# Turning the convolution's products round: conv matrices as the stationary side, result by channel

## The chip, the cores and the metric

One core of one Trainium2 chip. The metric is device time in microseconds (us), the median of several executions. The kernel before took 2316.77 us in the median of 3 runs (2316.7 to 2318.37).

## The reference, cut to what matters

64 graphs of 256 nodes with 256 channels, all in f32, go through a gated graph layer and a second graph layer. The part that the change touches is the convolution branch of the first layer:

```python
xc = jnp.transpose(x, (0, 2, 1))
h = jax.nn.relu(_bn(_conv1d(xc, conv1_w, 0), bn1_g, bn1_b, bn1_m, bn1_v))
h = _bn(_conv1d(h, conv2_w, 8), bn2_g, bn2_b, bn2_m, bn2_v)      # 17 taps
x_conv = jnp.transpose(jax.nn.relu(h + xc), (0, 2, 1))
s = x @ w_se.T + b_se                                            # distances, messages ...
A = jnp.exp(-dist) * mask
msg = jax.nn.relu(x @ w_msg.T + b_msg)
...                                                              # gates (GRU) on [x_conv, A @ msg], norm, second layer
```

## The kernel before

The 17-tap convolution is done for eight elements at once, as a transform on VectorE, 47 products of 256 x 256 with prepared matrices `w2m` on TensorE, and an inverse transform on VectorE. The data stand on the stationary side, so the result has positions on the partitions. The gates need channels there, so after x was added the result was transposed on TensorE, and ScalarE's relu wrote it to `xc`:

```python
def product(ps, slot, w, m):
    for c in range(C):
        nc.tensor.matmul(ps, X[:, slot, c * P:(c + 1) * P], w(m, c), start=(c == 0), stop=(c == C - 1))
...
def products(b, first, sums):                  # one group: 6 products into three PSUM banks
    p1, p2, p3 = bank("ps_k1"), bank("ps_k2"), bank("ps_k3")
    ...
    def take():                                # the group's evacuation
        k1 = sl(sums, 2).rearrange("p s e -> p (s e)")
        nc.scalar.copy(k1, p1)
        nc.vector.tensor_sub(..., k1, p3)
        nc.vector.tensor_add(..., k1, p2)
    return take
...
# the tail of conv(b)
before = []
for q in range(4):
    xb = x_by_tiles(b, q)
    nc.vector.tensor_add(sl(V + 4 * q, 4), sl(V + 4 * q, 4), xb)
    yield cost(4)
    yield None
    before.append(channels(q))                 # 8 transposes, 4 relus, two times "yield 1.0"
    if len(before) > 2:
        yield from before.pop(0)
...
```

The convolution of block b+1 is put between the work of the elements of block b. `conv` is a generator. Each `yield` says what the step just emitted counts for. Ten times in each element, 80 times in a block, `pump` draws steps from it until the sum drawn has reached its share of `total`, which is what all the steps of one block sum to:

```python
POINTS = 10
...
done, at, goal = 0.0, 0, BG * POINTS - 6

def pump():
    nonlocal done, at
    at += 1
    while done < total * at / goal:
        t = next(coming, 1e9)
        if t is None:
            break
        done += t

for k in range(b * BG, (b + 1) * BG):
    ...
    project(k - 1)
    step(up)                    # state update, part 1: two DVE operations, tanh
    pump()
    distances(k + 2)
    step(up)                    # part 2: three 128x512 operations and the norm's statistics on DVE
    pump()
    messages(k + 3)
    step(up)
    pump()
    ...
```

These calls emit each engine's instructions in this order, and the traces show what hangs on it: in the changed kernel a subtraction on DVE (L394, shown below) started 4.7 us after the copy that it needs was done, behind the part of a state update that stood before it.

## Time and profile before

| | per steady block (730.6 to 1003.2 us) | share |
|---|---|---|
| block | 272.6 us | |
| TensorE (PE) busy | 269.5 us | 99% |
| VectorE (DVE) busy | 208.5 us | 76% |
| ScalarE (ACT) busy | 89.8 us | 33% |

How to read it: a block lasts from the first gate of its first element (the first matmul of `ps_rz`) to that of the next. In the trace of before these gates start at 190.2, 458.8, 730.6, 1003.2, 1275.7, 1547.1, 1818.3 and 2089.9 us. So the front takes 190.2, seven blocks take 271.4 on average, and the last block, which carries no convolution, takes 224.7 to the end.

### The profile page before, as it was taken

What the parts mean: (1) busy time and instruction counts of PE and PEld (TensorE: products, weight loads), DVE (VectorE), ACT (ScalarE), POOL (GpSimd) and SP (SyncE); (2) the same over time, 40 slices, a digit from 0 to 9 for tenths busy, and PEclk for the clock granted to TensorE, in tenths of its full rate; (3) what the DMA queues carried; (4) which work ended last, traced back from release to release, by engine and by line L of the source; (5) the groups of instructions that cost most, each with busy time, mean ns of one, the idle gap of its engine ahead of it and who ended that gap; (6) DMA issues with size and microseconds to landing.
All of it is one profiled execution on the core that took longest, in us unless ns stands there. A gap on an engine that the chain in (4) does not pass through costs nothing.

```text
span 2314.6 us, 24215 instructions
## 1 busy us (share of the span) xinstructions
PE 2225.2 (96%) x8262; PEld 1456.2 (63%) x8262; DVE 1685.2 (73%) x3212; ACT 766.0 (33%) x1577; POOL 468.7 (20%) x925
## 2 busy tenths in 40 slices
PE   7879999999999999999999999999999999999996
PEld 4565566666666666666666566665666656666663
DVE  2893998759794788829887498956889398874543
ACT  4514222442224321353224332253223532243332
POOL 1000221312122222202212131221222122121211
PEclk8998999999999999999999999999999999999998
DMA  5543152224323144221532234222433214321100
GB/s 176 156 161 114 59 170 67 85 94 130 118 73 109 50 137 132 74 100 37 169 99 73 101 106 143 75 96 69 136 105 101 94 43 151 113 78 37 46 23 14
DMA packets 211128, 226.66 MB, mean 98 GB/s; under 512 B 22087, under 2 KB 201790, under 8 KB 211006
## 3 DMA queue, kind: packets, MB, share of 16 engines
q1 hardware_dynamic: 188448, 191.14, 26.2%
q10 hardware_dynamic: 22558, 33.99, 4.2%
q8 instruction: 66, 1.08, 0.2%
q14 instruction: 56, 0.46, 0.1%
HBM read 179.22 MB, written 45.88 MB: 97 GB/s over the span
## 4 chain that ended last, share of the span: by engine, by line
PE 69%; DVE 21%; DMA 4%; issue 3%; POOL 2%; ACT 1%; ACTq 0%; SPq 0%; DVEq 0%; POOLq 0%
PE ps_rz L637 14%; PE ps_k L383 12%; DVE XF L103 8%; PE ps_n L649 7%; PE ps_rz L635 7%; PE ps_out L712 6%; PE ps_c L454 5%; PE ps_nmp L619 4%; PE ps_n L647 4%; PE ps_out L724 3%; PE ps_msg L575 3%; DVE w L103 2%; DVE XF L464 2%; DVE bst L654 2%; DMA w<-w2m 2%
## 5 line engine op out<-in xcount | busy, mean ns | idle before, releaser
L103 DVE SCALAR_TENSOR_TENSOR XF<-XF 128x512 f32<-128x512 f32 (+2 forms) x800 | 506.7, 664 | 7.0
L676 POOL TENSOR_SCALAR q<-mv 128x2 f32<-128x2 f32 x64 | 32.1, 502 | 1459.1 <-DVE mv L655 1459.1
L383 PE MATMUL ps_k<-w,XF 128*128 128x256 f32 x1316 | 302.1, 385 | 15.2 <-ACT AT L609 11.6
L383 PEld LDWEIGHTS ps_k<-w,XF 128*128 128x128 f32 x1316 | 248.5, 192 | 64.1 <-ACT AT L609 17.3
L650 DVE TENSOR_TENSOR gn<-ps_n,brzn 128x512 f32<-128x512 f32 x128 | 88.1, 688 | 239.4 <-PE ps_n L649 239.4
L641 ACT ACTIVATE rz<-rz 128x512 f32<-128x512 f32 x128 | 80.7, 631 | 509.9 <-DVE rz L640 509.9
L635 PE MATMUL ps_rz<-whh,xT 128*128 128x512 f32 x512 | 240.8, 592 | 0.0
L637 PE MATMUL ps_rz<-wih,xc 128*128 128x512 f32 x512 | 240.6, 592 | 0.0
L637 PE MATMUL ps_rz<-wih,nmp 128*128 128x512 f32 x512 | 240.6, 592 | 0.0
L712 PE MATMUL ps_out<-wrr,hT 128*128 128x512 f32 x512 | 232.8, 598 | 5.5 <-ACT hT L701 5.5
L640 DVE TENSOR_TENSOR rz<-ps_rz,brzn 128x512 f32<-128x512 f32 x128 | 87.2, 681 | 192.2 <-PE ps_rz L637 192.2
L637 PEld LDWEIGHTS ps_rz<-wih,nmp 128*128 128x128 f32 x512 | 97.3, 190 | 122.5 <-issue 122.5
L637 PEld LDWEIGHTS ps_rz<-wih,xc 128*128 128x128 f32 x512 | 97.2, 190 | 122.5 <-issue 121.5
L712 PEld LDWEIGHTS ps_out<-wrr,hT 128*128 128x128 f32 x512 | 98.1, 192 | 105.2 <-issue 89.6
L580 ACT ACTIVATE msg<-msg 128x512 f32<-128x512 f32 x64 | 40.4, 631 | 353.1 <-DVE msg L579 353.1
L575 PE MATMUL ps_msg<-wms,xT 128*128 128x260 f32 x512 | 134.1, 402 | 12.5 <-DMA adj<-in_adjT_dram 8.1
L635 PEld LDWEIGHTS ps_rz<-whh,xT 128*128 128x128 f32 x512 | 92.2, 190 | 64.5 <-issue 61.2
L647 PE MATMUL ps_n<-whh,xT 128*128 128x256 f32 x512 | 131.6, 379 | 0.0
L649 PE MATMUL ps_n<-wih,xc 128*128 128x256 f32 x512 | 131.4, 379 | 0.0
L649 PE MATMUL ps_n<-wih,nmp 128*128 128x256 f32 x512 | 131.4, 379 | 0.0
L360 DVE TENSOR_TENSOR XF<-XF 128x512 f32<-128x512 f32 (+3 forms) x128 | 125.2, 1004 | 1.8
L454 PE MATMUL ps_c<-xTc,w 128*128 128x512 f32 x256 | 118.1, 604 | 7.6 <-ACT xTc L446 7.6
(105 smaller groups left out, 3486.6 us busy)
## 6 DMA issues: line engine op xcount, KB each, us to landing
w<-w2m SPq DMA_DIRECT2D x105, 768.0 KB, 5.9
xn<-in_x_dram SPq DMA_DIRECT2D x32, 512.0 KB, 4.3
xt<-xTc ACTq DMA_DIRECT2D x32, 512.0 KB, 3.3
xT<-xt SPq DMA_DIRECT2D x64, 256.0 KB, 3.0
adj<-in_adjT_dram SPq DMA_DIRECT2D x64, 256.0 KB, 2.8
x<-in_x_dram SPq DMA_DIRECT2D x64, 256.0 KB, 3.1
xb<-in_x_dram SPq DMA_DIRECT2D x32, 512.0 KB, 4.9
out_dram<-y ACTq DMA_DIRECT2D x64, 256.0 KB, 2.2
```

Source lines behind the costliest of these rows:

```text
L103: nc.vector.scalar_tensor_tensor(o, in0, s, in1, op0=op0, op1=op1)
L360: (nc.vector.tensor_add if add else nc.vector.tensor_sub)(sl(o, n), sl(a, n), sl(b, n))
L383: nc.tensor.matmul(ps, X[:, slot, c * P:(c + 1) * P], w(m, c), start=(c == 0), stop=(c == C - 1))
L454: nc.tensor.matmul(ps, w1[:, c, o * P:(o + 1) * P], xTc[:, c, :], start=(c == 0), stop=(c == C - 1))
L575: nc.tensor.matmul(ps[:, :D + 4], XT[k][:, c, m * P:(m + 1) * P], wms[:, c, :], start=(c == 0), stop=(c == C - 1))
L619: nc.tensor.matmul(ps[:, d * N:(d + 1) * N], MSG[k][:, m, d * P:(d + 1) * P], AT[k][:, m, :], start=(m == 0), stop=(m == C - 1))
L635: nc.tensor.matmul(prz, XT[k][:, c, q], whh[:, c, 0:2 * D], start=(c == 0), stop=False)
L637: nc.tensor.matmul(prz, t, wih[:, i, 0:2 * D], start=False, stop=(i == 3))
L647: nc.tensor.matmul(pn[:, D:], XT[k][:, c, q], whh[:, c, 2 * D:], start=(c == 0), stop=(c == C - 1))
L649: nc.tensor.matmul(pn[:, :D], t, wih[:, i, 2 * D:], start=(i == 0), stop=(i == 3))
L650: nc.vector.tensor_add(RZ[k][1][:, n, :], pn, brzn[:, 2 * D:])
L712: nc.tensor.matmul(ps, hT[:, c, n * P:(n + 1) * P], wrr[:, c, :], start=(c == 0), stop=(c == C - 1))
```

## The change

Its intent: put the conv matrix on the stationary side and the data on the moving side. Then the product comes out with channels on the partitions, and the 256 transposes of the result are not needed. x is added from the copy that already lies transposed in DRAM, and the batch norm's shift becomes the bias of the relu.

```diff
     def product(ps, slot, w, m):
-        for c in range(C):
-            nc.tensor.matmul(ps, X[:, slot, c * P:(c + 1) * P], w(m, c), start=(c == 0), stop=(c == C - 1))
+        for o in range(C):
+            q = slice(o * P, (o + 1) * P)
+            for c in range(C):
+                nc.tensor.matmul(ps[:, q], w(m, c)[:, q], X[:, slot, c * P:(c + 1) * P],
+                                 start=(c == 0), stop=(c == C - 1))
 ...
-                for j in range(4):
-                    nc.tensor.transpose(ps[:, j * P:(j + 1) * P], X[:, V + 4 * q + j, o * P:(o + 1) * P], ident)
-                ...
-                yield 1.0
-        before = []
-        for q in range(4): ...
+        def add_x(pair):
+            xb = conv_pool.tile([P, C, 2 * N], F32, tag="xb", name="xb")
+            nc.sync.dma_start(out=xb, in_=xt_dram[b * BG // 2 + pair])
+            v = view[:, :, :, pair * 2 * M:(pair + 1) * 2 * M]
+            nc.vector.tensor_add(v, v, xb.rearrange("p c (r j) -> p j c r", j=M))
+            yield cost(4)
+        def channels(pair):
+            for o in range(C):
+                nc.scalar.activation(xcs[h][:, o, g:g + 2]..., view[...], AF.Relu, bias=bn_shift[1][:, o:o + 1])
+        for pair in range(BG // 2):
+            yield from add_x(pair)
+            channels(pair)
 ...   (cut: x_by_tiles, the shift's row and its add in last_products)
```

The eight `yield 1.0` went with the transposes. They stood for 8 of the 107.7 units in `total`.

More of the change, by code (lines that the diff above doesn't have):

```diff
@@ L113, in weight @@
         return t
-    def x_by_tiles(b, q):
-        t = conv_pool.tile([P, 4, D], F32, tag="xb", name="xb")
-        nc.sync.dma_start(
-            out=t, in_=x[b * BG:(b + 1) * BG].rearrange("g (t j) d -> (g t) j d", j=M)[:, 4 * q:4 * q + 4, :])
-        return t
     chan_sb = const.tile([P, 8, C], F32)
@@ L139, in gnn_two_layers @@
     bn_scale, bn_shift = [], []
-    bn2_row = const.tile([P, 2, D], F32)
+    bn2_row = const.tile([P, D], F32)
     def batch_norms():
@@ L155, in along_rows @@
     def along_rows(pool):
-        for i, v in enumerate((bn_scale[1], bn_shift[1])):
-            ps = bank("ps_row")
-            for c in range(C):
-                dg = pool.tile([P, P], F32, tag="dg", name="dg", bufs=4)
-                nc.vector.tensor_scalar(dg, ident, v[:, c:c + 1], None, ALU.mult)
-                nc.tensor.matmul(ps[:, c * P:(c + 1) * P], ones, dg, start=True, stop=True)
-            nc.scalar.copy(bn2_row[:, i, :], ps[:, :D])
+        ps = bank("ps_row")
+        for c in range(C):
+            dg = pool.tile([P, P], F32, tag="dg", name="dg", bufs=2)
+            nc.vector.tensor_scalar(dg, ident, bn_scale[1][:, c:c + 1], None, ALU.mult)
+            nc.tensor.matmul(ps[:, c * P:(c + 1) * P], ones, dg, start=True, stop=True)
+        nc.scalar.copy(bn2_row, ps[:, :D])
     w2m = tc.dram_tile([NM, C, P, D], F32, name="w2m")
@@ L192, in scaled @@
                 ws[:, :n], WT[i][:, :, o - o0:o - o0 + n * OB].rearrange("p k (b o) -> p b k o", o=OB),
-                bn2_row[:, 0, o:o + n * OB].rearrange("p (b o) -> p b o", o=OB).unsqueeze(2)
+                bn2_row[:, o:o + n * OB].rearrange("p (b o) -> p b o", o=OB).unsqueeze(2)
                 .to_broadcast([P, n, TAPS, OB]))
@@ L381, in product @@
     def product(ps, slot, w, m):
-        for c in range(C):
-            nc.tensor.matmul(ps, X[:, slot, c * P:(c + 1) * P], w(m, c), start=(c == 0), stop=(c == C - 1))
+        for o in range(C):
+            q = slice(o * P, (o + 1) * P)
+            for c in range(C):
+                nc.tensor.matmul(ps[:, q], w(m, c)[:, q], X[:, slot, c * P:(c + 1) * P],
+                                 start=(c == 0), stop=(c == C - 1))
     def products(b, first, sums):
@@ L415, in take @@
             nc.scalar.copy(X[:, S2 + 6, :], p1[:, :D])
-            nc.scalar.copy(X[:, U + 1, :], p3[:, D:])
+            nc.scalar.copy(X[:, U:U + 2, :].rearrange("p s e -> p (s e)"), p3)
             nc.vector.tensor_sub(X[:, U + 2, :], X[:, S2 + 6, :], p2[:, :D])
             nc.vector.tensor_add(X[:, U + 3, :], X[:, S2 + 6, :], p1[:, D:])
-            nc.vector.tensor_add(X[:, U, :], p3[:, :D], bn2_row[:, 1, :])
         return take
@@ L522, in conv @@
         xcs = [work.tile([P, C, 4, N], F32, tag="xc", name="xc", bufs=3) for _ in range(2)]
-        def channels(q):
-            for o in range(C):
-                ps = bank("ps_xc")
-                for j in range(4):
-                    nc.tensor.transpose(ps[:, j * P:(j + 1) * P], X[:, V + 4 * q + j, o * P:(o + 1) * P], ident)
-                pv = ps.rearrange("p (j g t) -> p j g t", j=4, g=BG)
-                for h in range(2):
-                    nc.scalar.activation(
-                        xcs[h][:, o].rearrange("p g (t j) -> p j g t", j=M)[:, 4 * q:4 * q + 4],
-                        pv[:, :, 4 * h:4 * h + 4, :], AF.Relu)
-                yield 1.0
-        before = []
-        for q in range(4):
-            xb = x_by_tiles(b, q)
-            nc.vector.tensor_add(sl(V + 4 * q, 4), sl(V + 4 * q, 4), xb)
-            yield cost(4)
-            yield None
-            before.append(channels(q))
-            if len(before) > 2:
-                yield from before.pop(0)
-        for c_ in before:
-            yield None
-            yield from c_
+        view = X[:, V:V + M].rearrange("p j (c r t) -> p j c (r t)", c=C, r=BG)
+        def add_x(pair):
[5 more added lines that the diff above has]
+        def channels(pair):
+            h, g = pair // 2, 2 * (pair % 2)
+            for o in range(C):
+                nc.scalar.activation(
+                    xcs[h][:, o, g:g + 2].rearrange("p g (t j) -> p j g t", j=M),
+                    view[:, :, o, pair * 2 * M:(pair + 1) * 2 * M].rearrange("p j (g t) -> p j g t", g=2),
+                    AF.Relu, bias=bn_shift[1][:, o:o + 1])
+        for pair in range(BG // 2):
+            yield from add_x(pair)
+            channels(pair)
         for g in range(BG):
```

## The prediction

> **What bounds the kernel now.** I read the busy table of the page first, then the table by stretches, then the groups by shape on TensorE, then the order of time at three places.
>
> ```profile
> PE 2225.2 (96%) x8262; PEld 1456.2 (63%) x8262; DVE 1685.2 (73%) x3212; ACT 766.0 (33%) x1577; POOL 468.7 (20%) x925
> ```
>
> The average says TensorE (PE), with VectorE (DVE) a clear second. The kernel is eight convolution blocks, one for each eight batch elements, and block b+1 is woven into the elements of block b. So I cut the span where the transposes of the convolution result begin, which comes once per block:
>
> ```profile
> core 0: us, PE busy (x) PEld busy (x) DVE busy (x) ACT busy (x) POOL busy (x), PEclk, DMA share, GB/s
> 155.00:427.00 272.00, 251.72 (x926) 165.14 (x927) 215.29 (x399) 81.52 (x169) 53.20 (x97) 0.96 0.34 110
> 427.00:699.00 272.00, 268.24 (x1007) 175.60 (x1006) 208.59 (x398) 90.13 (x186) 60.08 (x114) 1.00 0.32 100
> ...
> 1787.00:2059.00 272.00, 268.39 (x1007) 175.68 (x1006) 208.65 (x398) 89.82 (x185) 60.08 (x114) 1.00 0.31 100
> ```
>
> A steady block takes 272 us, PE is busy in 268 of them, DVE in 209, ACT in 90. The stretch before 427 holds the one transition where PE is short of work. "Busy" is modelled for a pipelined engine, so I check it by the distance from one start to the next: two rows of the timeline, divided by the count.
>
> ```profile
> 1001.48 1.89 PE L724 MATMUL ps_out<-hr,adj 128*128 128x256 f32 x8
> 1003.21 1.02 PE L635 MATMUL ps_rz<-whh,xT 128*128 128x512 f32 x2
> ...
> 699.81 1.04 PE L528 MATMUL ps_xc<-ident,XF 128*128 128x128 f32 x8
> 700.68 1.68 PE L724 MATMUL ps_out<-hr,adj 128*128 128x256 f32 x7
> ```
>
> A 256-column f32 record takes (1003.21 - 1001.48) / 8 = 0.216 us; a transpose record with 128 columns takes (700.68 - 699.81) / 8 = 0.109 us. Every product is two records: the 94 product matmuls of a block (47 products, two halves of the contraction) show as 188. Counting all records of blocks 1 to 6 at such distances gives 1598 us of 1631, so at most 33 us (2%) in six blocks are gaps. A microsecond of PE work taken out of a block is therefore a microsecond of time, as long as nothing replaces it.
>
> [...] The scale rows of the batch norm are true f32 products of 128 by 128 with 128 moving columns, each with its own load, and they stand beside eight transposes[...]:
>
> ```profile
> 5.13 1.94 PE L445 MATMUL ps_xTc<-ident,xn 128*128 128x128 f32 x8 [5.13 <-POOL bnsc L148]
> 7.42 1.94 PE L162 MATMUL ps_row<-dg,ones 128*128 128x128 f32 x8 [0.36 <-DVE dg L161]
> ```
>
> Eight take 1.94 us in both. The full-weight products run at the transposes' pace, so I take 0.109 us for the new products at full clock. The sample is eight records.
>
> [...] In the trace the relu that writes every 16th element shows 628 ns for 256 elements, the exponential that writes them side by side (L609) 466[...]; for VectorE no instruction here reads f32 at a step of 64 bytes. [...] the add of x shows 1214.
>
> **The change part by part.**
>
> ```profile
> L383 PE MATMUL ps_k<-w,XF 128*128 128x256 f32 x1316 | 302.1, 385 | 15.2 <-ACT AT L609 11.6 <-DMA w<-w2m 2.5 <-DVE XF L300 0.6
> L528 PE MATMUL ps_xc<-ident,XF 128*128 128x128 f32 x256 | 34.1, 278 | 3.1 <-DVE XF L539 3.1
> L539 DVE TENSOR_TENSOR XF<-XF,xb 128x1024 f32<-128x1024 f32 x32 | 38.9, 1214 | 2.9 <-DMA xb<-in_x_dram 2.9
> L531 ACT ACTIVATE xc<-ps_xc 128x256 f32<-128x256 f32 x128 | 60.7, 628 | 5.9 <-ACT y L740 3.2 <-PE ps_xc L528 2.7
> ```
>
> Products: 188 records of 256 columns in a block become 376 of 128, 188 x (2 x 0.109 - 0.216) = +0.4 us[...]. Columns streamed stay the same; only weight loads double.
>
> Transposes: 32 of 0.109 us leave each block, -3.5 us of PE.
>
> Net on PE in a steady block -3.0 us, on the path. Blocks 1 to 7: 7 x 3.0 = -21 us.
>
> ScalarE: 16 relus at a pace of 60.7/128 = 0.47 us become 8 of 512 elements. My estimate is 631 (the tanh of 512 from SBUF) + 512 x (628 - 466)/256 = 0.95 us: 7.6 us a block before and after. Not on the path.
>
> VectorE: the four adds of x stay, but one operand (the transposed x) is read at a step of 64 bytes. At 1.2 us nothing changes; at twice that +4.9 us in a block where DVE has 63 idle. One add of 0.42 us goes (the shift moves into the bias of the relu).
>
> DMA: the same 512 KB four times a block, from the transposed copy already in DRAM.
>
> Order of work: the built program shows the adds now waiting for a transfer only, and the relu for DVE only. The convolution's own pacing sum falls from 107.7 to 99.7 units, because the eight steps for transposes no longer count, so its DVE work is spread over a few per cent more of the block. It still ends six of the eighty points before the block, about 20 us early.
>
> The front is the other gain:
>
> ```profile
> 175.15 3.75 PE L619 MATMUL ps_nmp<-AT,msg 128*128 128x256 f32 x8 [1.11 <-DVE AT L612]
> 181.10 1.94 PE L528 MATMUL ps_xc<-ident,XF 128*128 128x128 f32 x8 [2.20 <-DVE XF L539]
> 182.83 3.67 PE L575 MATMUL ps_msg<-wms,xT 128*128 128x260 f32 x8
> 186.30 2.06 PE L528 MATMUL ps_xc<-ident,XF 128*128 128x128 f32 x16
> 189.29 1.06 PE L528 MATMUL ps_xc<-ident,XF 128*128 128x128 f32 x8 [0.93 <-DVE XF L539]
> 190.19 1.88 PE L635 MATMUL ps_rz<-whh,xT 128*128 128x512 f32 x4
> ```
>
> In block 0 the first gate (L635) needs all four adds, because each add covers four columns j of every element; the fourth starts at 187.92 after its transfer. After the change an add covers a pair of elements, and the first gate needs the relus of the first pairs, whose adds start at 179.74 and 181.47. The messages product can start at 179 instead of 182.8 and the gate's own part near 183; the relu of the second pair should end near 185, against 191.9 for the first matmul on xc now. That is 6 to 7 us, of which I expect PE to lose 1 to 2 again waiting for x of the next block, whose transfers queue behind the same adds. I count -5. The products of block 0 add 0.5.
>
> Sum: 2316.8 - 21 - 5 + 0.5 = 2291 us.
>
> **The rivals.** First, the weight load shows. [...] For it: PEld is busy 63% already[...]. Against it: the eight records above, and that a load starts with the previous matmul throughout this trace[...].
>
> Second, PE gains, but a wait takes it back: DVE work lies at other places against the products (PE waits for ps_k already 15.2 us in all), or slow strided adds push the block's end. DVE's 63 us of slack speak against more than some us; that would be 2300 to 2312.
>
> Third, the front gains nothing, as its end is set by the transfers of x, four of 512 KB through two buffers: 2296.
>
> **Range and chances.** The steady part is arithmetic on measured distances; its size is 0.9% of the time, so even with the front doubled the gain stays near 1.4%. I take 2279 to 2305. Faster by over 2% would need 46 us, twice the transposes' whole cost: 0.04. Slower by over 2% is the first rival: 0.04. Within 2%: 0.92.
>
> **What would show it.** Products at a start-to-start distance of 0.109 us; a steady block of 269 us; no transposes, and PE busy about 265 of it; relus near 0.95 us and adds between 1.2 and 2.4; the first gate on xc near 185 to 187 us. A distance of 0.13 or more in the products would break the prediction, and so would new PE gaps of several us in a block with DVE named as the releaser.

## The result, and the profile after

The changed kernel took 2376.32 us (2373.45 to 2377.64, 4 runs); the kernel before, on the same chip, 2316.82. The ratio is 1.0254, with a 95% interval of 1.0236 to 1.0271. A ratio is the mean time of one kernel's runs over that of the other's in the same rounds, so it is not quite the ratio of the medians that are quoted. The result is correct, and it is slower by 2.5%. The prediction (2291) was wrong.

Where the time came from is read off the starts of the blocks. After the change they are 179.4, 460.2, 743.1, 1023.3, 1306.2, 1585.8, 1865.6 and 2147.0 us, and the last block takes 224.7. The front gained 10.8 us. The seven blocks lost 67.9 us together, 9.7 each.

The table by stretches for one block of after, with the same columns as in the prediction:

```profile
743.10:1023.30 280.20, 270.39 (x1162) 183.34 (x1161) 209.70 (x394) 90.22 (x177) 60.88 (x111) 0.98 0.31 97
```

PE is busy for 270 of 280 us, as long as before, although the transposes are gone. DVE (208.5 before) and ACT (89.8) do hardly more. So the time went into gaps, and into something that counts as busy. The groups whose work changed, by shape (busy us, mean ns of one, idle before):

```profile
L377 PE MATMUL ps_k<-XF,w 128*128 128x128 f32 x2632 | 323.4, 285 | 55.1 <-DVE XF L394 22.9 <-DMA w<-w2m 17.8 <-ACT XF L393 8.4
...
L524 DVE TENSOR_TENSOR XF<-XF,xb 128x1024 f32<-128x1024 f32 x32 | 61.0, 1925 | 18.1 <-DMA xb<-xt 18.0
L530 ACT ACTIVATE xc<-XF,bnsh 128x512 f32<-128x512 f32 x64 | 67.6, 1155 | 20.4 <-DVE XF L524 17.2 <-ACT y L730 3.2
```

The add takes 1.925 us (1.214 before) and a relu 1.155 (0.95 was estimated). The products' idle time rose from 15.2 to 55.1 us; its largest releaser is new, and the wait for weights grew from 2.5 to 17.8 us. The list of waits on PE names a fourth one (us in total, times, longest):

```profile
PE ps_k L377 <- DVE XF L394: 22.9, 7, 3.3
PE ps_dist L597 <- ACT lr L588: 20.7, 9, 2.8
...
PE ps_k L377 <- DMA w<-w2m: 17.8, 10, 3.1
```

"7 times" means once in each block that carries a convolution. Here is one case of each of these three in the order of time, in the block from 743 to 1023 (start, us, engine, operation). First, the wait for DVE:

```profile
919.97 1.95 PE L377 MATMUL ps_k<-XF,w 128*128 128x128 f32 x16
...
920.63 0.69 DVE L657 TENSOR_TENSOR w<-x,nn 128x512 f32<-128x512 f32 x1
...
924.47 0.68 DVE L394 TENSOR_TENSOR XF<-XF,ps_k 128x512 f32<-128x512 f32 x1
...
925.20 5.47 PE L377 MATMUL ps_k<-XF,w 128*128 128x128 f32 x32 [3.28 <-DVE XF L394]
```

Sixteen records are two products. The third has to wait for the subtraction at L394, which reads the third bank of the group before (that it is this bank which must come free is inferred from the code; the releaser is what the trace shows). That subtraction (`take`) stands in DVE's queue behind part 2 of a state update, which begins with L657 at 920.63. PE idles 3.28 us. The copy that L394 needs was done on ACT at 919.78, and still L394 started 4.7 us later, behind the update.

And the 32 records after the gap take 5.30 us until the next group starts at 930.50. At the pace of an undisturbed burst they would take 32 x 0.1117 = 3.57. The table by stretches says why, in the third figure from the end, the granted clock (the share of its full speed that TensorE was given):

```profile
872.30:876.80 4.50, 4.50 (x40) 4.50 (x41) 4.33 (x10) 0.68 (x2) 0.00 (x0) 1.00 0.00 0
...
925.20:928.60 3.40, 3.40 (x21) 3.40 (x22) 3.40 (x10) 1.61 (x3) 2.90 (x8) 0.67 0.00 0
```

After the 3.28 us gap the granted clock drops to 0.67 in the next 3.4 us. The stretch from 872.3 follows a gap of 1.21 us, and there the clock stays at 1.00. Slow matmuls count as busy (3.40 of 3.40 us at a clock of 0.67), so "PE busy" hid a part of the loss.

The length of a gap alone does not decide it. Of the 20 gaps of over 2 us between 190 and 2147 us, 14 were followed by a fall of the clock to 0.50 and 6 were not, among them two of the same 3.28 us gaps, at 361.7 and 1484.7. All falls in this stretch begin on one grid of 3.41 us. Here are cells of that grid around the 2.31 us gap shown next, and around the 3.28 us gap at 361.7:

```profile
885.42:888.83 3.41, 1.10 (x9) 0.90 (x9) 3.38 (x8) 0.00 (x0) 2.55 (x4) 1.00 1.09 356
888.83:892.24 3.41, 3.41 (x19) 3.41 (x18) 1.60 (x3) 2.10 (x4) 0.00 (x0) 0.50 0.61 194
...
359.76:363.17 3.41, 1.96 (x17) 1.75 (x15) 3.24 (x8) 0.00 (x0) 0.00 (x0) 1.00 0.00 0
363.17:366.59 3.42, 1.59 (x14) 1.59 (x15) 3.39 (x11) 0.20 (x1) 2.38 (x6) 1.00 0.03 5
366.59:370.00 3.41, 3.41 (x28) 3.25 (x27) 3.09 (x7) 1.41 (x3) 2.02 (x4) 1.00 0.00 0
```

The shorter gap lay in one cell, which was idle for 2.31 us; the longer one was split, 1.45 and 1.83 us. In this trace every cell from 190 to 2147 us with 1.94 us of idle PE or more was followed by a fall, and of those with less only one, with 1.52. Idle time is not all that counts: in the trace of before a cell with 1.95 was not followed by a fall, and two with 1.12 were (865.84 and 1138.91; both held the distances' matmuls, which use 4 rows). What else counts stays open.

Second, the weights' transfer (SPq is the queue that issues it):

```profile
881.00 0.42 SPq L556 DMA_DIRECT2D x<-in_x_dram  x1
...
881.47 2.09 SPq L370 DMA_DIRECT2D w<-w2m  x3
...
887.96 7.22 PE L377 MATMUL ps_k<-XF,w 128*128 128x128 f32 x48 [2.31 <-DMA w<-w2m]
```

The transfers are issued right behind the loads of an element, the first one lands 6.4 us later (the median of all is 7.0), and PE waits. Here too the clock falls after the gap: the 48 records take 7.06 us until the next group starts, instead of 48 x 0.1117 = 5.36.

Third, the end of the block:

```profile
1014.11 2.09 ACT L530 ACTIVATE xc<-XF,bnsh 128x512 f32<-128x512 f32 x2
1016.01 0.61 ACT L611 COPY nmp<-ps_nmp 128x512 f32<-128x512 f32 x1
...
1016.99 0.35 ACT L588 COPY lr<-ps_sT 36x256 f32<-36x256 f32 x1
...
1017.39 0.70 PE L597 MATMUL ps_dist<-lr 4*128 4x256 f32 x4 [2.40 <-ACT lr L588]
1018.02 3.37 PE L565 MATMUL ps_msg<-wms,xT 128*128 128x260 f32 x8
```

The last relus stand in ACT's queue ahead of the copies of `nmp` and `lr`, and the distances of a later element need `lr`. Before the change the same copy and the same matmul were far apart, and the messages product behind them took 2.02 us at a granted clock of 1.00 (999.63 to 1001.48), where it takes 3.37 at 0.58 now (1018.02 to 1021.39):

```profile
994.19 0.35 ACT L598 COPY lr<-ps_sT 36x256 f32<-36x256 f32 x1
...
999.00 0.70 PE L607 MATMUL ps_dist<-lr 4*128 4x256 f32 x4
...
999.63 2.02 PE L575 MATMUL ps_msg<-wms,xT 128*128 128x260 f32 x8
```

The sum for this block, gap plus slow spell: 3.28 + 1.73 for the evacuation, 2.31 + 1.70 for the weights, 2.40 + 1.35 for the end, 12.8 us. A block lost 9.7 on average against before, where the change should have saved up to 3.0, so these three are about what has to be explained.

### The profile page after: what moved, and what is told of

Same layout as the page of the kernel before. It is cut to its first block, busy times and chain, and to the rows that moved or that the text cites. A ratio compares the mean times of both kernels' runs of the same rounds, so it can differ in the third digit from the quotient of the medians.

```text
span 2371.7 us, 26609 instructions
## 1 busy us (share of the span) xinstructions
PE 2227.7 (94%) x9506; PEld 1502.2 (63%) x9506; DVE 1704.5 (72%) x3202; ACT 772.9 (33%) x1512; POOL 480.5 (20%) x925
## 4 chain that ended last, share of the span: by engine, by line
PE 75%; DVE 14%; DMA 6%; ACT 2%; issue 2%; POOL 1%; SPq 0%; POOLq 0%; ACTq 0%; DVEq 0%
PE ps_rz L627 15%; PE ps_k L377 14%; PE ps_n L639 8%; PE ps_rz L625 7%; PE ps_out L702 5%; PE ps_c L447 5%; DVE XF L103 5%; PE ps_out L714 4%; PE ps_msg L565 4%; PE ps_nmp L609 4%; PE ps_n L637 4%; DMA w<-w2m 3%; DVE XF L524 2%; DMA xb<-xt 2%; PE ps_dist L597 1%
## 5 line engine op out<-in xcount | busy, mean ns | idle before, releaser
L377 PE MATMUL ps_k<-XF,w 128*128 128x128 f32 x2632 | 323.4, 285 | 55.1 <-DVE XF L394 22.9
L377 PEld LDWEIGHTS ps_k<-XF,w 128*128 128x128 f32 x2632 | 316.8, 200 | 72.9 <-issue 32.4
L666 POOL TENSOR_SCALAR q<-mv 128x2 f32<-128x2 f32 x64 | 38.9, 608 | 1471.4 <-DVE mv L645 1471.4
L565 PE MATMUL ps_msg<-wms,xT 128*128 128x260 f32 x512 | 141.7, 422 | 12.1 <-DMA adj<-in_adjT_dram 8.0
L703 ACT COPY hr<-ps_out 128x256 f32<-128x256 f32 x128 | 47.0, 373 | 261.8 <-PE ps_out L702 261.8
L565 PEld LDWEIGHTS ps_msg<-wms,xT 128*128 128x128 f32 x512 | 99.0, 204 | 48.1 <-issue 22.6
```

What stands on the lines that cost most here:

```text
L377: nc.tensor.matmul(ps[:, q], w(m, c)[:, q], X[:, slot, c * P:(c + 1) * P], start=(c == 0), stop=(c == C - 1))
L565: nc.tensor.matmul(ps[:, :D + 4], XT[k][:, c, m * P:(m + 1) * P], wms[:, c, :], start=(c == 0), stop=(c == C - 1))
```

## The experiments

The theory after reading this, A: the time is lost by the order of work, that is by the steps that no longer count in `total`. Its rivals: the new orientation of the products costs more than it seems; or the slow strided adds and relus cost the time wherever they stand. Where the records below use letters, A is the theory of the order, and A2 is the form of it in which the places of the product groups among the points of an element count, and not only how late the block's end lies; the other letters are rivals. In the end A came apart into three pieces: the evacuation behind the update, the late transfers of weights, and the late end.

Eighteen kernels ran, in five calls with their own runs of before (medians 2319.82, 2316.01, 2314.85, 2315.42 and 2315.97). For comparisons I use the ratios to before, times 2317 us.

### e1 and e2: the steps alone

e1 is the changed kernel with the old steps put back:

```diff
                     AF.Relu, bias=bn_shift[1][:, o:o + 1])
+                yield 1.0
+        before = []
         for pair in range(BG // 2):
             yield from add_x(pair)
-            channels(pair)
+            yield None
+            before.append(channels(pair))
+            if len(before) > 2: yield from before.pop(0)      # and the rest after the loop
```

> The changed kernel with the convolution's steps of before: each relu group counts 1.0 again, a break after each add, relus two adds late, so that every other instruction stands where it stood before. Theory A (the shifted interleaving makes PE wait): nearly all of the 9.7 us a block comes back, 2290 to 2305. Theory B (the slower adds of 1.9 us and relus of 1.16 us and the two buffers of x at the block's end make PE wait): the stall at the block's end stays, 2315 to 2340. Theory C (the new orientation of the products itself stalls PE): the stalls among the products stay, 2335 to 2365.

Measured: correct, 2300.69 us, ratio 0.9915 (0.990 to 0.9929).

e2 is the kernel before, transposes and all, with the steps of the changed kernel: the lines above taken out of it.

> The kernel before, right result, transposes and old products kept, but with the steps of the changed kernel: the transposes and relus count nothing and follow each add at once. Theory A: it becomes slower by 30 to 65 us, 2345 to 2380. Theories B and C: it stays within 10 us of 2317.

Measured: correct, 2425.53 us, ratio 1.0452 (1.0436 to 1.0469). The old products and plain adds lose 4.5% as soon as the steps go. Its list of waits has 23.3 us of the products for the evacuation's subtraction, as in the changed kernel, and 49.2 us of the transposes for the adds, which come right before them now. That is 45 us beyond the range that A had been given, as the transposes' new waits came on top. What follows: A holds, in both directions. The slow instructions can't be the whole, as e1 keeps every one of them.

### e3: the products alone

The kernel before with nothing but the new `product` (the first hunk of the change; a wrong result, since the transposes then turn it the wrong way).

> The kernel before with the new orientation of the products alone (wrong result on purpose: the result lies by channel and is then transposed as if it did not). By the pace seen after (0.1115 us against 0.216 for twice the columns) the products cost 1.3 us more a block: theories A and B say 2322 to 2332. Theory C says 2345 or more.

Measured: 2325.89 us, ratio 1.0019 (1.0002 to 1.0036), so +4.4 us with an interval from 0.5 to 8.3. The prediction's term was 8 x 0.4 = 3.2 us. At the old order of work the rival of the orientation falls.

### e4, e6, e7, e8: only the number

e4 is the changed kernel with one line added:

```diff
+    total += 8.0
     POINTS = 10
```

> The changed kernel with 8.0 added to the pacing sum, so that splits, products and merges are emitted at the old points and only the block's end differs (adds one per point and relus at once, but earlier). Theory A, as far as it lies among the products: the waits of ps_k (about 7 us a block with their slow clock) go, 2310 to 2330. Theory B: the block's end still stalls, and the products' waits too if they come from it, 2340 to 2375.

Measured: correct, 2293.12 us (2290.79 to 2295.16), ratio 0.9883 (0.9869 to 0.9898). This beats both kernels, it is better than either theory had said, and it lies 2 us from the predicted 2291. The adds still take 1.911 us, but the products wait as little as before:

```profile
L377 PE MATMUL ps_k<-XF,w 128*128 128x128 f32 x2632 | 311.5, 278 | 16.5 <-ACT AT L599 11.3 <-DMA w<-w2m 3.5 <-DVE XF L292 1.1
```

e6 adds 4.0 and e7 adds 16.0 instead; e8 is the kernel before with `total -= 8.0`.

> The changed kernel with 4.0 added instead of 8.0. Theory A1 (the later the convolution's work is emitted, the more waits, smoothly): halfway, 2325 to 2345. Theory A2 (waits appear only where a group of products falls next to the state update's chain on VectorE, or where the end comes too late): anything from 2290 to 2370, with the same waits of 3.3 us present or absent as a whole.

> The changed kernel with 16.0 added, faster emission than before. Theory A1: 2293 or a little less. Theory A2: new meetings of products and update, 2300 to 2360.

> The kernel before, all its steps kept, with 8.0 taken from the pacing sum alone. If the sum is the whole cause, transposes and their places aside: slower by 40 to 110 us, 2360 to 2425, with the same 3.3 us waits of ps_k for VectorE. If the loss of the second run came from the transposes following the adds at once: 2317 to 2340.

Measured: e6 2293.62 us (ratio 0.9904), e7 2377.36 (1.0262, 17 us above the wider of its two ranges), e8 2372.05 (1.0244). The kernel before, with every transpose and plain add in place, gets as slow as the changed one by this number alone, and its list shows the same wait:

```profile
L383 PE MATMUL ps_k<-w,XF 128*128 128x256 f32 x1316 | 324.2, 406 | 56.0 <-DVE XF L399 23.3 <-DMA w<-w2m 15.8 <-ACT XF L398 8.7
```

What follows: the time is not monotone in the number. With 99.7 units it is 2376, with 103.7 and 107.7 it is 2293, with 115.7 it is 2377. So the number does not act by being large or small. That it acts by where the steps fall among the ten points of an element is the reading that fits; e9, e17 and the trace of e7 below support it. And "a larger share of the block is better" would be the wrong lesson.

### e5, e12, e13: the late end alone

e5 uses 107.7 units while the products run, and 99.7 from the inverse transform on:

```diff
-            while done < total * at / goal:
+            while done < (total + (0.0 if STAGE.get(b + 1) == "inverse" else 8.0)) * at / goal:
```

> The changed kernel with the pacing sum raised by 8.0 until the last merges begin and left at 99.7 from there: the products stand at the old points, the end of each block (adds of x, relus) at the late points of the changed kernel. Against the rate-only kernel (2293) it prices the late end alone. If the end accounts for the wait of the distance product and its spell of slow clock (some 4 us a block in the trace after): 2318 to 2330. If all the loss lies among the products: 2290 to 2300.

Measured: correct, 2319.85 us, ratio 1.0014 (0.9998 to 1.0031). The wait of the distances is back (20.1 us in 9 times), those of the products are not, and its list shows no other new wait. Against e4 (0.9883) that is 0.0131 x 2317 = 30 us for the late end alone. But is it the end that costs, or the slow instructions in it? e12 is e5 with the transposed x read side by side, and e13 is e5 with the relu writing side by side (both give a wrong result):

```diff
-            nc.vector.tensor_add(v, v, xb.rearrange("p c (r j) -> p j c r", j=M))
+            nc.vector.tensor_add(v, v, xb.rearrange("p c (j r) -> p j c r", j=M))        # e12
```

```diff
-                    xcs[h][:, o, g:g + 2].rearrange("p g (t j) -> p j g t", j=M), ...
+                    xcs[h][:, o, g:g + 2].rearrange("p g n -> p (g n)").rearrange("p (j q) -> p j q", j=M), ...   # e13
```

> The kernel with the late end only (2319.85), with the transposed x read side by side in the add: wrong result on purpose, same bytes and same steps. The add should fall from 1.91 us to about 1.2. If the slow add makes the late end costly, the wait of the distances for the lr copy (20.1 us) shrinks by more than half and the time comes to 2300 to 2308. If the queue of relus on ACT or the late end itself does, the wait stays and the time is within 5 us of 2319.

> The kernel with the late end only (2319.85), with the relus writing side by side instead of every 16th element: wrong result on purpose, same steps. A relu should fall from 1.155 us to 0.6 to 0.8, so the two of a pair from 2.1 to about 1.4. If the relus ahead of the nmp and lr copies in ACT's queue make the wait of the distances, the wait falls by about 0.7 us each time (20.1 to about 14 or less) and with fewer half-clock spells the time comes to 2300 to 2312. If not, it stays within 5 us of 2319.

Measured: e12 2296.81 us, ratio 0.9925; e13 2309.62, ratio 0.9978. In e12:

```profile
L597 PE MATMUL ps_dist<-lr 4*128 4x256 f32 x256 | 45.4, 431 | 8.6 <-ACT lr L588 8.6
...
L524 DVE TENSOR_TENSOR XF<-XF,xb 128x1024 f32<-128x1024 f32 x32 | 38.5, 1222 | 22.9 <-DMA xb<-xt 22.9
```

The plain add gives back 0.0089 x 2317 = 21 us of the 30 (a little more than expected), and the plain relu (712 ns for 1157) 8 us. So the rival of the slow instructions is right in part: where the end is late, the slow add is worth 21 us; e4, where the end is early, has the same slow add and is still 0.0042 x 2317 = 10 us faster than e12. Two attempts to soften the late end by more buffers for the transposed x failed in the build; what buffers would do stays open, though the adds wait 17.0 us for these transfers in e5 and 1.6 in e4.

"Late end" is a short name, and lateness itself is not what costs. In e7, with 115.7 units, the last relu ends at 991.57, 34 us before the block's first gate at 1025.85, and the distances wait even longer, 30.4 us in all; the same neighbours meet, one element earlier:

```profile
989.49 2.08 ACT L530 ACTIVATE xc<-XF,bnsh 128x512 f32<-128x512 f32 x2
991.39 0.61 ACT L611 COPY nmp<-ps_nmp 128x512 f32<-128x512 f32 x1
...
992.76 1.22 PE L597 MATMUL ps_dist<-lr 4*128 4x256 f32 x4 [4.00 <-ACT lr L588]
```

And in e1, with the old steps between adds and relus, the last relu ends only 5.4 us before the gate, with 4.5 us of that wait in all. What costs is that the last relus hold up the copies queued right behind them; in these runs it did not matter when in the block that happened.

### e9, e10: the order of evacuation and update

e9 is the changed kernel with 99.7 units and the evacuation of a finished group ahead of part 2 of the update:

```diff
-            take = make()
+            PEND.append(make())
 ...
-            take()
+            flush()                 # runs what is in PEND, once
 ...
                 distances(k + 2)
+            flush()
             step(up)
```

> The changed kernel with its sum of 99.7 untouched; only the DVE and ACT evacuation of a finished product group is put ahead of the second part of the state update of the same element, instead of behind it. If the 3.3 us waits of the products are the evacuation standing behind the update's chain on DVE, the wait of ps_k for the subtraction (22.9 us, 7 times) and the half-clock spells after it go, worth about 22.9 + 7 x 1.7 = 35 us: 2335 to 2350, and no long wait for that subtraction in the list. If the loss comes from elsewhere (weights' transfers, the adds, the relus), the time stays at 2365 to 2376. The distance wait at the end of the block (20.7 us) should stay in both.

Measured: correct, 2342.74 us, ratio 1.0118 (1.0101 to 1.0135). The wait for L394 is gone from the list. (1.0254 - 1.0118) x 2317 = 32 us: the order is shown. The size fits as well: 22.9 us of gaps, and a slow spell of 1.7 us behind five of the seven, make 31. What is left in e9 is the distances' wait (24.9 us), and the waits of the products for weights (15.5) and for rz on DVE (7.7).

e10 is the same with 16 more units.

> The same edit with the sum raised by 16, where the time was 2377.36. If the order of evacuation and update makes the ps_k wait (17.6 us) there as well, it goes and some 25 us come back: 2345 to 2360. The waits of the distances and messages at the block's end, which the order does not touch, should stay, so that it is still slower than before. If nothing comes back (2370 to 2380), the order is not what makes the loss at this sum.

Measured: correct, 2343.36 us, ratio 1.0122. It gained (1.0262 - 1.0122) x 2317 = 32 us from 2377, a little more than expected, and the distances' wait stayed (33.0 us).

### e14, e15: an attempt that decided nothing

e14 is the mirror of e5 (the 8 units are added from the inverse transform on, so the end is early again), e15 adds the evacuation first.

> The mirror of the run with the late end only: the sum stays at 99.7 while the products run, and 8 is added from the merges on, so that the block's end comes as early as in the good kernel. If late end (27 us) and the rest (56 us) simply add, the time is 2376 - 27 = 2349, with the wait of ps_k for the subtraction (22.9 us) kept and the wait of the distances gone. If the early products alone make the loss and the end only follows from them, it stays above 2365.

> The same with the evacuation ahead of the update's second part. If the three parts add, 2349 - 34 = 2315, which leaves some 22 us that neither explains, with the waits for the weights' transfers (15.5 us) as the largest left. If order and late end together are the whole loss, 2293 to 2300.

Measured: e14 2387.24 us, ratio 1.0307; e15 2360.75, ratio 1.0195. Both missed. The distances' wait went, as it should (20.7 us to 2.8), but the sudden jump in the sum puts some seven units of work (an estimate from the sum) into one place, and new waits appeared: 20.0 us of `ps_out` for `hT` in e14, where it was 5.5. That the lump made them is likely and not shown. The two runs say nothing on whether the parts add; between them the order is worth (1.0307 - 1.0195) x 2317 = 26 us, near the 32 above.

### e17, e18: the rest of the sum

e17 is e9 with each weights' transfer issued one step earlier:

```diff
-        nc.sync.dma_start(out=t[:, :n], in_=w2m[first:first + n]...)
+        for i in range(first // 3, min(first // 3 + 2, 16)):      # this one and the next
+            if (b, i) not in AHEAD:
+                t = work.tile([P, 3, C, D], F32, tag="w2", name="w2", bufs=3)
+                nc.sync.dma_start(out=t[:, :k], in_=w2m[3 * i:3 * i + k]...)
+                AHEAD[b, i] = t
```

> The run with the evacuation first (2342.74) and each transfer of weights issued one step earlier in SP's queue (a transfer of 768 KB lands 7.0 us after its issue, and in that run some were issued just before their products, behind loads of the elements). If late weights are the third part, the waits for w (15.5 us) and most of those for rz (7.7) go with their half-clock spells: 2315 to 2327, with the wait of the distances (24.9 us) kept. If the transfers are late for another reason, 2338 to 2346.

Measured: correct, 2313.27 us, ratio 0.9992 (0.9976 to 1.0009); (1.0118 - 0.9992) x 2317 = 29 us, slightly more than expected. The products wait 11.5 us in all, and 2.9 of it for weights:

```profile
L389 PE MATMUL ps_k<-XF,w 128*128 128x128 f32 x2632 | 306.0, 276 | 11.5 <-ACT XF L405 8.4 <-DMA w<-w2m 2.9
```

e18 is e17 with the plain add of e12 (wrong).

> The same with the transposed x read side by side in the add (wrong result on purpose), which was worth 23 us where only the end was late. If order, late weights and the slow add at a late end are the three parts, they add up: 2292 to 2304, as near the good kernel as if the sum had been raised. If something else is left, it stays above 2308.

Measured: 2293.69 us, ratio 0.9900 (0.9885 to 0.9914); another (0.9992 - 0.9900) x 2317 = 21 us. With 99.7 units untouched, three edits that each take away one wait bring the changed kernel from 2376 to 2294 (the last of them at the price of the result). That is the sum: order 32, weights 29, slow add at a late end 21, together 82 us. e4 lies at 0.9883, so 4 us are left, within the intervals. Each edit was priced only on top of the ones before it, so the split into 32, 29 and 21 belongs to this order of edits; the earlier transfers alone were not run.

### e16, e19: a version that beats both

e16 is e4 with the evacuation first, e19 has the earlier transfers as well.

> The good kernel (sum raised by 8, 2293.12) with the evacuation ahead of the update's second part. There no group waits for its evacuation, so the order should be worth nothing: 2288 to 2298. If it gains more than 5 us, the order is a gain of its own; if it loses, moving it ahead delays the update, and the 34 us of the changed kernel were a net of more than the wait.

> The best version so far (2285.84) with the earlier transfers. It waits 2.5 us for w in all, so the edit can give 3 us at most: 2282 to 2290. A loss would mean that the earlier transfers hold up the loads of the elements behind them in SP's queue.

Measured: e16 2285.84 us, ratio 0.9875 (0.9857 to 0.9892), which can't be told from e4's 0.9883 (2 us under the range expected). e19 2279.97 us (2278.87 to 2281.67), ratio 0.9843 (0.9828 to 0.9858), correct: the best of all, 1.6% under the kernel before. It gained more from the earlier transfers than the wait of 2.5 us had promised, about 7 us, and came out 2 us under its range; why is open.

## Why the prediction was wrong, point by point

**The bound** was right. TensorE bounds the kernel (busy in 269.5 of a block's 272.6 us), and a microsecond of it is a microsecond of time (in e9, gaps and slow spells of 31 us went, and 32 us of time). What followed from it was not drawn: then a microsecond in which it waits is one too.

**Products** were right. The extra cost was 4.4 us in e3 against the predicted 3.2. The trace's pace is (861.23 - 854.75) / 58 = 0.1117 us where 0.109 was taken. The first rival never came near: with twice the weight loads (2632 for 1316) a record still started every 0.1117 us. But the ground was thinner than it read. The eight records ran at 1.94 / 8 = 0.2425 us each, 2.2 times the 0.109 that was taken (eight transposes at 181.10 take the same 1.94 us, at a granted clock of 0.50), and their loads showed 324 ns in the mean where those of the products (L383) showed 192, so they could not settle the pace of 0.109; and a load that stood alone took 190 ns in the trace of before (L635 at 1003.64), longer than such a record. By the pace the products cost 376 x 0.1117 - 188 x 0.216 = 1.4 us more in a block, not 0.4; over eight blocks that is 11 us, more than e3 measured in all; why is open. The net of -3.0 us a block and the 0.5 us for block 0 were estimates: the distances in the prediction give -3.1 and 0.4.

**Transposes and the steady block** held only once the pacing was mended. Then a block takes 269.8 us on average in e4 against the predicted 269. Measured from the mean of before (271.4), it saved 1.6 and not 3.0; the products' 1.4 explain most of the difference.

**The front** was right in its mechanism and half the size: the first gate started 10.8 us earlier in the changed kernel (10.3 in e4), where 5 was counted. It did not have to wait for the second pair, as the prediction had it: its matmul on xc started at 181.11, when the relus of the second pair had not begun (181.98). In e4, 7 x 1.6 + 10.3 = 21.5 us was saved; the two errors of size cancelled in part, and by that luck the predicted 2291 stands so near the 2293 of e4.

**Relus and adds** came out longer than the estimate (1.155 for 0.95) and inside the range (1.925). But "not on the path" and "DVE has 63 idle" failed at the end of the block: there the slow add cost 21 us in all (e18 against e17, e12 against e5).

**The step that failed** is "Order of work": "The convolution's own pacing sum falls from 107.7 to 99.7 units [...] so its DVE work is spread over a few per cent more of the block. It still ends six of the eighty points before the block, about 20 us early." The number was seen and taken for harmless. The runs show in its place that this number alone is worth (1.0254 - 0.9883) x 2317 = 86 us (e4), and that it costs the kernel before 56 us as well (e8). It set three things at once: a group's evacuation fell behind the state update on DVE (32 us), its weights were issued behind an element's loads (29 us), and the last adds and relus came just ahead of ACT's copies for the distances (21 us). "About 20 us early" was not even so in the trace of before: its last relu ended at 993.4, only 9.8 us ahead of the gate at 1003.2. After the change it was 1023.3 - 1016.2 = 7.1 us, and the copy at L588 was needed before that.

**The second rival** named the cause ("a wait takes it back: DVE work lies at other places against the products"), but gave it 2300 to 2312. Its argument was an average: 63 us of DVE's slack in a block. Slack in the block doesn't help a subtraction that has to come within two products. The gaps are not the whole size: from 460.2 to 2147.0, six blocks, PE idles 66.0 us where it was 20.4, and is busy 10 us longer (1620.8 for 1610.7) although transposes worth 21 us are gone and the products grew by 8. So slow clock made up about a third of the loss, which is an estimate from these figures.

**What would show it** did its work: "new PE gaps of several us in a block with DVE named as the releaser" is the first line of the waits.

## What to carry to other kernels

Where a generator is woven into other work by counted steps, the counts are part of the kernel: when a change drops a step, hold the sum fixed first and measure the change alone, then try a few sums, since the time need not be monotone in them. Judge slack at the place where a result is needed, by the order of instructions on the engine that gives it (here L394 started 4.7 us after its operand was done, behind an update), and not by an engine's idle share of a block (24% for DVE before). When PE is the bound, look behind each new gap of about 2 us and more for a slow spell too, which the page shows as busy time: here 14 of 20 such gaps had one, worth some 1.4 to 1.7 us at the three places measured.

## What the traces and runs show of the clock, the products and the 64-byte step

- In the trace of after, gaps of 2.31 and 2.40 us on PE were followed by a fall of the granted clock from 1.00 to 0.50: 48 records then took 7.06 us for 5.36, and a messages product 3.37 for 2.02. A gap of 1.21 us left the clock at 1.00. The falls from 190 to 2147 us lie on a grid of 3.41 us, and 2.31 us of idle inside one cell of it were followed by a fall, where a 3.28 us gap split into 1.45 and 1.83 was not.
- f32 records of 128 columns with a full load each ran at 111.7 ns, while the loads themselves show 200 ns in the mean (L377 of after).
- An f32 add on VectorE of 1024 elements with one operand at a step of 64 bytes took 1925 ns (1927 in e5), against 1222 ns read side by side (e12, which is e5 with that one change). A relu on ScalarE of 512 elements took 1157 ns writing at that step (e5), and 712 side by side (e13).
